# Three order tables of a decoder layer's kernel, arranged anew

## The chip, the cores and the metric

The kernel runs on one core of a Trainium2 chip. A core has a matrix engine (TensorE, "PE" in the profile, with its weight loads shown as "PEld"), a vector engine (VectorE, "DVE"), an activation engine (ScalarE, "ACT"), a general engine (GpSimd, "POOL") and a queue for transfers (SyncE, "SP"). Each runs its own list of instructions in the order in which the program recorded them; they meet at semaphores. The metric is the device time of one execution in microseconds (us).

## The reference

One decoder layer with norms after each part, all in 32-bit floats: 8 sequences of 112 tokens, width 256; a context of 375 rows per sequence.

```
x = layernorm(x + self_attention(x))                # 16 heads of 64
x = layernorm(x + cross_attention(x, ctx, mask))    # 16 heads of 16, 375 keys
x = layernorm(x + moe(x) + shared(x))               # 8 experts, the best one per token

self_attention:  softmax(q k^T / 8) v, then w_out and b_out
cross_attention: softmax(where(mask == 0, -1e10, q k^T / 4)) v, then Wo and bo
moe:    silu(x gate_e^T) * (x up_e^T) down_e^T with e = argmax(x router^T)
shared: the same form with one set of weights for every token
```

## The kernel before

**The work of one sequence** is cut into parts, and each part has a short word. A step `s` (there are 9) runs three sequences at different places: the self attention of sequence `s` (small letters), the cross attention of sequence `s-1` (capitals), and the end of the cross attention of `s-2` (`F1` to `F6`). Between them stand projection pieces for later steps, which depend on nothing that is close in time. The words, with the lines of the code:

| word | part | lines | TensorE's work in it |
|---|---|---|---|
| s0, s1 | self scores of 8 heads, row maxima | 332 | 16 matmuls on 64 rows of the array (row tiles) |
| e0, e1 | subtract the maximum (VectorE), exp (ScalarE) | 350 | none |
| w0, w1 | row sums and reciprocal (VectorE), product (POOL) | 356 | none |
| t00 to t11 | transposes of the self weights, 4 heads, and a copy | 363 | 4, full array |
| v0, v1 | weights times values, and a copy | 371 | 16 on 64 columns (column tiles) |
| o, n | output projection, sum, statistics; normalize | 384, 393 | 16, full |
| q1, q2 | transposes of the normed row block; queries | 406, 410 | 2 and 8, full |
| S0 to S3 | cross scores of 4 heads, minimum and exp of heads 0 and 1 | 433 | 8 on 32 rows |
| E0 to E3 | the same minimum and exp for heads 2 and 3 | 457 | none |
| T00 to T32 | transposes of the cross weights (group, third of the keys), a copy | 460 | 4, full |
| V0 to V3 | cross weights times values, a copy | 470 | 24 on 32 columns |
| F1 to F6 | transposes and division; transposes; output projection, sum, statistics; normalize; transposes for the experts; router scores | 488 to 523 | 4, 2, 4, 0, 2, 4, full |
| k0 to k7 | queries and keys of a pair of sequences | 259 | 8, full |
| u0 to u3 | values of a sequence | 283 | 4, full |
| c0, c1 and c2 to c4 | keys and values of a context | 299 | 4 each, full |
| a0 to a3, b0 to b3 | gate and up of the shared expert, first half of the tokens | 611 | 4 each, full |
| r, R, z | routing on VectorE; ranks and scatter; constants | 666, 680, 214 | R has 4, full |

The counts are those of the profile, where each 32-bit matmul stands twice. A tile that spans all rows and columns of the array is called full here; the others take 32 or 64 rows, or 32 or 64 columns, and put several matmuls side by side.

**The order** is written by hand. The scheduler is off (`tc.manual_schedule()`), and three strings hold the words: `FIRST` for step 0, `STEP` for steps 1 to 7, `LAST` for step 8. The function `step` (lines 532 to 547) reads a string word by word and records the instructions of each part on all engines:

```
for word in table.split():
    on = word[-1] if word[-1] in "+-" else ""
    word = word.strip("+-")
    if word in pieces:
        pieces.pop(word)(on)
        continue
    what, arg = word[0], [int(d) for d in word[1:]]
    whose = {"F": old, "q": crosses.get(s)}.get(what, cross if what in "SETV" else own)
    if whose is not None and what in PARTS:
        getattr(whose, PARTS[what])(on, *arg)
```

A word that has no sequence or piece in a step is left out: no `F` in step 1, no `k` in steps 6 and 7, no `u` in step 7. The sign behind a word says which engine copies the result out of PSUM (line 245): `+` is VectorE, none or `-` is ScalarE. For queries (`k0`, `k2`) and context keys it is always ScalarE, for context values always VectorE.

**Buffers.** Three pools of PSUM have two tiles each: `sc` (scores; S takes both, s one), `pt` (all transposes) and `mm` (all other matmuls). So each group of matmuls waits until the tile of the group but one before it, in its pool, has been read out. The weights `pr`, `ex` and their transposes are doubled too.

**Transfers** are issued on SP in the order of the program. Those that the words touch: the context of the next sequence, at the start of each step, once the buffer's last reader, a `c` piece of the step before, is done; and the weights of the shared expert, after step 7, into memory that the self attention has left.

After step 8 come the end of the last cross attention, the second half of the shared expert, the routing, and nine tiles of experts (from line 708); the tables don't touch them.

Of the kernel before, what the change touches and what calls it, by code (L numbers as in the profile page):

```python
# [25 lines left out]


STEP = """
S0 c0 E0 F1 s0 c1 T00- T01- e0 S1 w0 F2 T02- E1 c2 s1 V0- T10- t00- e1 F3 T12- T11- c3 F4 c4 t01- w1
V1- F5 S2 k0 u0- t10- E2 t11+ S3 v0+ v1+ E3 T20+ T21+ o T22- T30+ F6 u1- k1+ T32- k3- V2- n q1 T31+  # L30
k2 q2 V3+
"""
FIRST = """
k5+ s0 e0 k7+ k6 w0 k4 u2+ s1 t00+ e1 u3+ t01+ k0 w1 c0 u1- v0+ c1 t10+ t11+ k2 v1+ o k1+ n c2 c3 z
q1 u0- q2 k3+ c4
"""
LAST = """
S0 E0 F1 a0- b0- F2 T00+ S1 E1 T01- T02+ F3 a1+ F4 T10- V0+ T12- T11- S2 V1- b1- F5 E2 b3- a2- r
T20- R T22- S3 E3 b2- T21+ a3- T30+ T31+ F6 T32+ V2+ V3+
"""  # L40


# [919 lines left out]
```

## Time and profile before

| | |
|---|---|
| median of 3 runs | 432.33 us (431.8 to 432.77) |
| the profiled execution, its own time | 431.49 us |
| its span, from the first to the last instruction | 429.7 us |
| granted clock of TensorE, mean | 0.992 |
| step 0 (from the first matmul at 5.0) | to 48.6 us |
| step 1 | 48.6 to 86.7 us |
| steps 2 to 5, each | 39.7 us |
| step 6 | 245.6 to 279.5 us |
| step 7 | 279.5 to 311.5 us |
| step 8 | 311.5 to 338.3 us |
| the rest | 338.3 to 429.7 us |

A step is counted from the first matmul of its `S0` to that of the next. The page has these costliest groups (line, engine, operation, out<-in, shapes, count; busy time, mean length in ns; idle time before it on its engine and who ended it):

```profile
L455 ACT ACTIVATE ex<-ex,nm 112x375 f32<-112x375 f32 x128 | 70.5, 601 | 47.8 <-DVE nm L451 47.1
L451 DVE CUSTOM_DVE_ANT_0 ex<-sc,cap 112x375 f32<-112x375 f32 x128 | 63.2, 542 | 19.4 <-PE sc L439 19.4
L465 PE MATMUL pt<-ident,ex 112*125 112x112 f32 x384 | 55.9, 278 | 0.3
L361 POOL TENSOR_TENSOR pr<-pr,den 112x896 f32<-112x896 f32 x16 | 26.9, 1682 | 127.9 <-ACT exT L247 71.9
L247 ACT COPY exT<-pt 125x448 f32<-125x448 f32 x62 | 31.3, 530 | 30.4 <-PE pt L465 30.4
...
L247 DVE COPY exT<-pt 125x448 f32<-125x448 f32 x34 | 20.4, 618 | 19.1 <-PE pt L465 19.0
```

A line is that of the code, or of a helper: every copy out of PSUM has line 247, every plain product line 251. The length of a matmul is modelled and overlaps the next one, so for TensorE the distance from start to start is read, not the sum of lengths. Idle time of an engine that isn't the bound costs nothing.

### The profile page before, as it was taken

The numbers are of one execution on the slowest core, as the hardware profiler recorded it, in microseconds if no ns is written. First come the engines' busy times: TensorE is split into PE (matmuls) and PEld (weight loads), VectorE is DVE, ScalarE is ACT, GpSimd is POOL, SyncE is SP. The second block draws the span as 40 slices with busy tenths as digits, with TensorE's granted clock in tenths as the row PEclk, the third lists the DMA queues.
The fourth block names the chain that finished last, engine by engine and source line by source line (L and its number), as shares of the span: only waits on it lengthen the run. The fifth ranks groups of instructions, "written<-read, shape, count | busy, mean of one in ns | idle before, by whom it ended". The sixth has DMA issues, their size and how long they took to land.

```text
span 429.7 us, 8390 instructions
## 1 busy us (share of the span) xinstructions
PE 411.0 (96%) x3378; PEld 318.7 (74%) x3378; DVE 244.5 (57%) x676; ACT 182.2 (42%) x365; POOL 87.6 (20%) x117
## 2 busy tenths in 40 slices
PE   5999999999999999999999999998999899999990
PEld 4968677877787787778777776766865665899990
DVE  0554676387638655863785387588675745106442
ACT  1221375366437634752664286366356501111110
POOL 3030012103001200221040012113100515713334
PEclk9999999999999999999999999999999999999996
DMA  8970390001000100010010000000395204179700
GB/s 278 300 203 0 116 273 30 1 2 37 2 0 2 38 2 0 4 36 2 1 37 2 2 2 0 2 2 2 122 400 215 66 15 147 32 260 384 271 24 24
DMA packets 27372, 35.80 MB, mean 83 GB/s; under 512 B 2448, under 2 KB 20191, under 8 KB 27330
## 3 DMA queue, kind: packets, MB, share of 16 engines
q1 hardware_dynamic: 25202, 31.94, 22.9%
q0 software_dynamic: 1584, 2.76, 2.0%
q8 instruction: 28, 0.46, 0.4%
q10 hardware_dynamic: 544, 0.52, 0.3%
q14 instruction: 14, 0.11, 0.1%
HBM read 28.78 MB, written 7.62 MB: 85 GB/s over the span
## 4 chain that ended last, share of the span: by engine, by line
PE 94%; DVE 1%; DMA 1%; POOL 1%; issue 1%; ACT 1%; POOLq 0%
PE mm L251 49%; PE pt L465 11%; PE sc L251 10%; PE sc L439 6%; PE mm L476 5%; PE sc L339 3%; PE mm L375 3%; PE pt L368 3%; PE pt L242 2%; DMA wq<-in_w_qkv 1%; PE pt L492 1%; PE pt L823 0%; POOL pr L361 0%; DVE ex L451 0%; POOL rs L232 0%
## 5 line engine op out<-in xcount | busy, mean ns | idle before, releaser
L455 ACT ACTIVATE ex<-ex,nm 112x375 f32<-112x375 f32 x128 | 70.5, 601 | 47.8 <-DVE nm L451 47.1
L451 DVE CUSTOM_DVE_ANT_0 ex<-sc,cap 112x375 f32<-112x375 f32 x128 | 63.2, 542 | 19.4 <-PE sc L439 19.4
L465 PEld LDWEIGHTS pt<-ident,ex 112*125 112x125 f32 x384 | 49.9, 189 | 10.0 <-issue 2.8
L465 PE MATMUL pt<-ident,ex 112*125 112x112 f32 x384 | 55.9, 278 | 0.3
L361 POOL TENSOR_TENSOR pr<-pr,den 112x896 f32<-112x896 f32 x16 | 26.9, 1682 | 127.9 <-ACT exT L247 71.9
L247 ACT COPY exT<-pt 125x448 f32<-125x448 f32 x62 | 31.3, 530 | 30.4 <-PE pt L465 30.4
L232 POOL TENSOR_TENSOR rs<-rs,mhalf 112x1 f32<-112x1 f32 (+1 forms) x25 | 14.3, 571 | 144.3 <-DVE rs L231 144.2
L251 PE MATMUL mm<-xT_sb,wq 128*128 128x224 f32 x128 | 29.0, 373 | 5.0 <-DMA wq<-in_w_qkv 5.0
L247 DVE COPY exT<-pt 125x448 f32<-125x448 f32 x34 | 20.4, 618 | 19.1 <-PE pt L465 19.0
L251 PE MATMUL mm<-wv,xT_sb 128*112 128x512 f32 x64 | 30.5, 599 | 0.0
L251 PEld LDWEIGHTS mm<-xT_sb,wq 128*128 128x128 f32 x128 | 24.3, 199 | 8.0 <-DMA wq<-in_w_qkv 5.0
L439 PE MATMUL sc<-kc,qz 32*112 32x375 f32 x256 | 29.8, 519 | 0.0
L251 PE MATMUL mm<-wo,aoT 128*112 128x256 f32 x128 | 29.0, 380 | 0.0
L251 PE MATMUL mm<-xT_sb,wk 128*128 128x224 f32 x128 | 27.8, 363 | 0.0
L251 PEld LDWEIGHTS mm<-xT_sb,wk 128*128 128x128 f32 x128 | 24.6, 197 | 2.8 <-issue 2.2
L251 PEld LDWEIGHTS mm<-wo,aoT 128*112 128x112 f32 x128 | 22.1, 177 | 4.5
L476 PE MATMUL mm<-exT,vc 125*32 125x112 f32 x768 | 24.8, 263 | 0.0
L251 PE MATMUL mm<-cT,wxk 128*128 128x375 f32 x64 | 24.4, 503 | 0.0
L251 PE MATMUL mm<-wxv,cT 128*125 128x256 f32 x96 | 23.6, 382 | 0.0
L247 DVE COPY kT<-mm 128x448 f32<-128x448 f32 x11 | 6.9, 623 | 25.4 <-PE mm L251 25.4
L354 ACT ACTIVATE pr<-pr 112x896 f32<-112x896 f32 x16 | 15.4, 960 | 13.3 <-DVE pr L353 13.3
L476 PEld LDWEIGHTS mm<-exT,vc 125*32 125x32 f32 x768 | 17.4, 110 | 4.9 <-issue 1.9
(160 smaller groups left out, 664.4 us busy)
## 6 DMA issues: line engine op xcount, KB each, us to landing
wg<-in_gateT SPq DMA_DIRECT2D x9, 512.0 KB, 9.7
wu<-in_upT SPq DMA_DIRECT2D x9, 512.0 KB, 10.5
wd<-in_downT SPq DMA_DIRECT2D x9, 512.0 KB, 10.0
cT<-in_ctxT SPq DMA_DIRECT2D x8, 375.0 KB, 3.3
xs_d<-fill_sb SPq DMA_DIRECT2D x1, 1799.0 KB
zs_d<-fill_sb SPq DMA_DIRECT2D x1, 1792.0 KB
wv<-in_w_qkv SPq DMA_DIRECT2D x2, 512.0 KB
wo<-in_w_out SPq DMA_DIRECT2D x1, 1024.0 KB
```

What stands on the lines that cost most here:

```text
L232: G.tensor_tensor(rs[:n], rs[:n], mhalf[:n], ALU.pow)
L247: (V.tensor_copy if on == "+" else A.copy)(dst, src)
L251: nc.tensor.matmul(out_, lhsT, rhs, start=(i == 0), stop=(i == len(pairs) - 1))
L339: nc.tensor.matmul(sc[:S, j, bass.ts(c, S)], qT[rows, 4 * g + c, self.tok], kT[rows, 4 * g + c, self.tok], start=True, stop=True,)
L354: A.activation(pr, pr, AF.Exp)
L361: G.tensor_tensor(pr, pr, den.unsqueeze(3).to_broadcast([S, 2, 4, S]), ALU.mult)
L368: nc.tensor.transpose(pt[:S, bass.ts(c, S)], self.pr[g][:, j, c, :], ident[:S, :S])
L439: nc.tensor.matmul(sc[i // 2][:S, i % 2, :S2], self.qz[rows, par, c, :], kc[rows, c, :], start=True, stop=True,)
L451: V.tensor_tensor_reduce(ex[:, i, :], self.sc[g][i // 2][:S, i % 2, :S2], cap, -1.0, BIG, ALU.add, ALU.min, nm[:, i : i + 1],)
L455: A.activation(ex[:, i, :], ex[:, i, :], AF.Exp, bias=nm[:, i : i + 1], scale=-1.0)
L465: nc.tensor.transpose(pt[:JT, bass.ts(i, S)], self.ex[g][:, i, bass.ts(t, JT)], ident[:S, :S])
L476: nc.tensor.matmul(av[32 * i : 32 * i + 32, 0:S], vcs[self.b % 2][:, t, 8 * c + 2 * i + par, :], self.exT[g][:, t, bass.ts(i, S)], start=( ...
```

## The change

Only the three strings change. The same words stand in each; their order is another, and some have another sign. In `STEP`, `v0`, `T21`, `T30` and `k1` go from `+` to `-`. In `FIRST`, `k5`, `u2`, `u3`, `v0`, `t11`, `k1` and `k3` go from `+` to `-` and `u1` from `-` to `+`. In `LAST`, `T02`, `a1` and `V0` go from `+` to `-`, and `b0`, `T10`, `V1` and `T20` from `-` to `+`.

```
 STEP = """
-S0 c0 E0 F1 s0 c1 T00- T01- e0 S1 w0 F2 T02- E1 c2 s1 V0- T10- t00- e1 F3 T12- T11- c3 F4 c4 t01- w1
-V1- F5 S2 k0 u0- t10- E2 t11+ S3 v0+ v1+ E3 T20+ T21+ o T22- T30+ F6 u1- k1+ T32- k3- V2- n q1 T31+
-k2 q2 V3+
+S0 c1 E0 s0 c0 T00- e0 k3- F1 S1 T01- T02- E1 c4 s1 V0- F2 e1 u1- w0 T10- c3 w1 T11- c2 T12- S2 V1-
+F3 t00- t01- u0- t10- E2 t11+ k0 v0- F4 v1+ S3 T20+ E3 F5 o T21- T22- F6 k2 T30- V2- n q1 T32- k1-
+T31+ q2 V3+
 """
 FIRST = """
-k5+ s0 e0 k7+ k6 w0 k4 u2+ s1 t00+ e1 u3+ t01+ k0 w1 c0 u1- v0+ c1 t10+ t11+ k2 v1+ o k1+ n c2 c3 z
-q1 u0- q2 k3+ c4
+k6 k5- k7+ u3- k4 s0 e0 s1 k2 e1 u1+ w1 w0 c1 u2- k1- k3- c0 t00+ t01+ c2 t10+ z t11- v0- v1+ o n
+u0- c3 q1 k0 q2 c4
 """
 LAST = """
-S0 E0 F1 a0- b0- F2 T00+ S1 E1 T01- T02+ F3 a1+ F4 T10- V0+ T12- T11- S2 V1- b1- F5 E2 b3- a2- r
-T20- R T22- S3 E3 b2- T21+ a3- T30+ T31+ F6 T32+ V2+ V3+
+S0 E0 b0+ a2- T00+ T02- S1 F1 T01- a0- E1 F2 b3- S2 b1- E2 T10+ F3 T11- a1- r T12- V0- V1+ F4 S3
+T20+ R T22- a3- E3 T21+ F5 b2- T30+ F6 T31+ T32+ V2+ V3+
 """
```

## The prediction, made before the changed kernel ran

> **What bounds the kernel now.** I read the page first (busy shares, chain), then the stretches of one step each, then one step in the timeline, TensorE alone and with all engines.
>
> ```profile
> span 429.7 us, 8390 instructions
> PE 411.0 (96%) x3378; PEld 318.7 (74%) x3378; DVE 244.5 (57%) x676; ACT 182.2 (42%) x365; POOL 87.6 (20%) x117
> PE 94%; DVE 1%; DMA 1%; POOL 1%; issue 1%; ACT 1%; POOLq 0%
> ```
>
> The chain of what ended last lies to 94% on TensorE, so time is won only by what TensorE does between matmuls. By stretches (columns: length; busy us and instructions of PE, PEld, DVE, ACT, POOL; clock; DMA share; GB/s):
>
> ```profile
> 166.10:205.80 39.70, 39.67 (x362) 30.58 (x358) 24.87 (x67) 21.14 (x43) 5.88 (x6) 1.00 0.04 11
> 245.60:279.50 33.90, 33.87 (x334) 24.75 (x330) 24.37 (x66) 19.47 (x40) 5.70 (x6) 1.00 0.00 1
> 279.50:311.50 32.00, 30.50 (x322) 23.36 (x318) 24.31 (x66) 18.50 (x38) 5.69 (x6) 1.00 0.13 42
> ```
>
> A full step takes 39.7 us with TensorE "busy" throughout, but busy is not peak: matmul ends are modelled and overlap. What counts is start to start, in TensorE's timeline (start, length, group):
>
> ```profile
> 131.41 1.02 PE L465 MATMUL pt<-ident,ex 112*125 112x112 f32 x8
> 132.36 1.04 PE L439 MATMUL sc<-kc,qz 32*112 32x375 f32 x8
> 133.34 0.41 PE L242 MATMUL pt<-ident,xo 112*128 112x112 f32 x2
> 134.99 1.04 PE L339 MATMUL sc<-kT,qT 64*112 64x112 f32 x16
> 135.96 0.78 PE L476 MATMUL mm<-exT,vc 125*32 125x112 f32 x24
> 136.68 0.97 PE L465 MATMUL pt<-ident,ex 112*125 112x112 f32 x4
> 137.55 0.59 PE L368 MATMUL pt<-ident,pr 112*112 112x112 f32 x4
> 138.84 1.03 PE L465 MATMUL pt<-ident,ex 112*125 112x112 f32 x8
> 139.71 1.90 PE L251 MATMUL mm<-wxv,cT 128*125 128x256 f32 x8
> 143.81 1.78 PE L251 MATMUL mm<-xT_sb,wq 128*128 128x224 f32 x8
> 145.43 1.88 PE L251 MATMUL mm<-wv,xT_sb 128*112 128x512 f32 x4
> 157.91 1.68 PE L251 MATMUL mm<-xT_sb,wk 128*128 128x224 f32 x8
> 159.42 0.59 PE L465 MATMUL pt<-ident,ex 112*125 112x112 f32 x4
> ```
>
> Two things are to be seen. First, the tile shape costs. Eight projection matmuls between full-array groups take 159.42-157.91 = 1.51 us; entered from a row-tiled group (143.81) they take 1.62: an entry costs 0.11. Leaving costs as much: all single starts around a change of shape show some 0.19 from the last matmul of 112 columns to the next shape's first, where the same shape gives 0.095. Second, eight transposes of ex take 139.71-138.84 = 0.87, so four take 0.44; the four at 136.68 take 0.87. The same moments with all engines:
>
> ```profile
> 134.35 1.08 DVE L359 TENSOR_REDUCE den<-pr 112x8 f32<-112x896 f32 x1
> 136.00 0.55 DVE L451 CUSTOM_DVE_ANT_0 ex<-sc,cap 112x375 f32<-112x375 f32 x1
> 136.12 1.11 ACT L455 ACTIVATE ex<-ex,nm 112x375 f32<-112x375 f32 x2 [0.35 <-DVE nm L451]
> 137.28 0.18 PEld L465 LDWEIGHTS pt<-ident,ex 112*125 112x125 f32 x1 [0.20 <-ACT ex L455]
> ...
> 298.31 0.98 PE L368 MATMUL pt<-ident,pr 112*112 112x112 f32 x8 [1.31 <-POOL pr L361]
> ```
>
> The word w0 (1.08 us of den on VectorE) stands ahead of E1, so the exps of heads 2 and 3 end at 137.23 and T10 has to wait; t00 right after it waits for POOL's product of the same w0. In step 7, which has no k and u pieces to fill, t10 waits 1.31 us for POOL.
>
> **What the Trainium skill says.** "TensorEngine Tiling (Array Packing)", Key Properties: a change of tiling mode, not of tile alone, drains TensorE. The trace agrees: 0.19 in place of 0.095 at each change. "TensorE: Matmul & The Clock Gate", Part 2, step 1: weight loads are pulled ahead of running matmuls, the matmuls keep their order; the page adds (Architectural detail) that ScalarE and VectorE are strict FIFO. Here too: the first pair after a change is longer by a weight load (0.42 against 0.315 for 375 columns), and E1 stands behind den.
>
> **The change part by part.** Arithmetic is unchanged: the same matmuls; by the order of instructions 31 PSUM copies go from VectorE to ScalarE (four in a full step: v0, T21, T30, k1). That is 4 x 0.53 = 2.1 us more on ScalarE (21.1 to 23.3 of 39) and 4 x 0.62 less on VectorE: free in total, only queue order matters.
>
> (a) Tile shapes. Counted in TensorE's order, changes of shape fall from 153 to 141: FIRST 8 to 4 (s0,s1 and v0,v1 become neighbours), six STEP steps by one, LAST by two. One change removed saves exit plus entry, 0.095 plus 0.06 to 0.11, taken as 0.18: 12 x 0.18 = 2.2 us.
>
> (b) w0, w1 go behind E1, u1 and T10, so E1 follows S1's own two heads. I laid the step out anew by adding the start-to-start durations of its groups (S 0.83, keys 1.37, s 0.97, k 1.51, u 1.72, V 0.71, o 3.46, two v 1.69, c vals 0.87, q2 0.97 and so on). From S0 = 0: s0 2.29, T00 4.63, S1 7.11, T01 7.93, c4 8.9, V0 10.8, T10 13.5, S2 16.65, F3 18.2, t00 19.1, u0 19.9, k0 22.4, v0 24.0, S3 25.7, o 27.2, V2 34.0, q1 34.7, T31 36.9, V3 38.3, end 39.04. Against it the producers in their queues: E1's second exp ends 11.7, T10 needs it at 13.5 (0.19 gone); w0's product ends on POOL at 16.3, w1's at 18.5, t00 comes at 19.1 and t10 at 21.6 (0.16 gone). S1 now lies 1.1 us later (7.11, before 132.36-126.34 = 6.0) and clears e0's subtraction (5.6), for which it took 0.98 in place of 0.83 (0.15 gone). So 0.5 us of waits go per step.
>
> (c) Key pieces and norm's steps moved later: c1/c0 swapped, k3 early, F2 to F6 shifted. Norm: o's sum ends 31.2, POOL's power 32.7, n 33.1, q1 at 34.7, covered. On SP only the context load is touched: it waits for the last c piece (now 16 us into a step, before about 15) and lands 3.3 us after issue, needed next step: free. The shared weights wait for o of step 7, land some 5 us after it, and b0 now comes first, 6.3 us after it: margin 1.3. FIRST asks for the second half of wv at about 18 us; SP's ring of semaphores shows it down at 12.6. POOL's queue keeps its kinds of work; the power for F3 comes behind both w products, at 20.6, with F4 at 23: free.
>
> (d) Tight places of the new order: v1 wants k0's PSUM buffer at 24.85, ScalarE frees it at 24.75; V0 wants T02's copy by 11.1, which stands behind S1's exps and ends 10.7; V3 wants T31's copy (38.1) at 38.3. Each lies between nothing and 0.2 us; below nothing it can't go, no work is shorter. I take 0.1 a step in all.
>
> Sum by stretch: FIRST -0.7 (four changes, no other wait before). Step 1: waits 0.15+0.68 (58.5 to 60), change 0.0, less 0.1: -0.75. Steps 2 to 5: 4 x (0.5+0.17-0.1) = -2.3. Step 6: 0.5, 0.16 (q2 behind x1T's copy), change 0.17, less 0.15 new (T31 behind q1's copy): -0.7. Step 7: before 0.5+1.38+0.24+0.16, change 0.17, less 1.0 new (T12 behind T10's copy 0.3; t10 behind t00's copy, which stands behind S2's exps, 0.5; T31 0.2): -1.5. LAST: -0.36 for changes, +0.3 because R, and with it POOL's scatters, come 1.4 us later and b2 is squeezed: -0.1. The tail from 338.3 is the same code and moves along. Sum -6.05. Own time of the profiled execution: 431.49, of which 429.7 is span; so 425.4. The median shown is 432.33, 0.84 above: 426.3.
>
> **Rivals.**
> 1. Only the shapes count: waits move, as exps and copies of ScalarE (2.1 us more per step) end late elsewhere. For: T01, T02 and V0 now stand behind S1's exps in ScalarE's FIFO, and step 7 shows how quickly a thin step waits. Against: ScalarE idles 16 us of a full step. Gain 2.2: 430.1.
> 2. Slower: ScalarE's queue between S1 and e1. T01's and T02's copies stand behind two exps; if VectorE's xo product and S1's maxima ahead of them come late, V0 (10.8) and, behind it, F2, u1 and T10 shift alike in every step. Margin 0.4 us; each further us costs 7 us over seven steps. To eat the gain of 6 takes 0.4+0.86 = 1.26 us of lateness; at 1.7 us, about three more ScalarE items ahead, the time is 432.33 + 7x1.3 - 6 = 435.4. Against: in the trace copies come 0.2 us after their matmuls and 0.41 apart.
> 3. Nothing: the changes of shape are paid but the weight load of the next group would have been exposed anyway, and waits move wholly. 432.3.
>
> **How the numbers follow.** Forecast, waits and changes gone: 0.66 (own range 424.6 to 428). Rival 1: 0.20. Rival 2: 0.09. Rival 3: 0.05. Predicted 426.3. The range 424.0 to 430.8 takes in rival 1's value and the unknown costs of (d), 0.2 us a step. What a measurement can tell from no change is 0.2%, 0.86 us. Faster 0.86, same 0.05, slower 0.09.
>
> **What would show it.** Right: stretches S0 to S0 near 39.1 (39.7), step 7 near 30.5, FIRST ending near 47.8 (48.6); four transposes of T10 in 0.5; no POOL wait over 1 us on TensorE. Wrong: any TensorE group in a full step that lasts 0.3 us over its duration above, above all V0, v1, V3 or T12; a step of 40 us or more; b0 waiting for a DMA.

## The result, and the profile after

The changed kernel takes **425.42 us** (median of 4 runs, 424.85 to 425.79), beside 432.15 us (4 runs, 431.8 to 432.77) of the kernel before: ratio 0.9842, 95% interval 0.9824 to 0.9859, so it is faster by 1.6%. The prediction was 426.3 us, faster. The profiled execution took 425.79 us, 5.7 less than that of before; its span is 424.1 us. The page of the changed kernel:

```profile
span 424.1 us, 8388 instructions
...
PE 406.5 (96%) x3378; PEld 316.6 (75%) x3378; DVE 227.9 (54%) x645; ACT 195.9 (46%) x396; POOL 89.1 (21%) x117
...
PE 94%; DVE 1%; DMA 1%; issue 1%; ACT 1%; POOL 1%; POOLq 0%; ACTq 0%
...
L247 ACT COPY exT<-pt 125x448 f32<-125x448 f32 x75 | 38.2, 528 | 17.8 <-PE pt L465 17.1
```

The chain still lies to 94% on TensorE with the same 3378 matmuls. VectorE has 31 instructions less and ScalarE 31 more: the copies whose sign changed (the `exT` copies on ScalarE go from 62 to 75). ScalarE is now 13.7 us busier, and the share of the chain on it is still 1%. The stretches of a full step, step 6 and step 7, in the columns used before:

```profile
163.30:202.40 39.10, 39.10 (x365) 30.25 (x360) 22.90 (x63) 22.86 (x47) 5.88 (x6) 1.00 0.04 11
241.50:275.10 33.60, 33.42 (x330) 24.57 (x326) 22.92 (x63) 20.67 (x43) 5.70 (x6) 1.00 0.00 1
275.10:306.30 31.20, 30.58 (x325) 23.25 (x321) 22.74 (x63) 19.60 (x41) 5.66 (x6) 1.00 0.14 49
```

From the first matmul of `S0` to the next one's:

| stretch | before | after | difference | predicted |
|---|---|---|---|---|
| to the first `S0` | 48.56 | 48.23 | -0.33 | -0.7 |
| of it, from the fifth `k` piece on | 34.97 | 34.29 | -0.68 | |
| step 1 | 38.05 | 36.97 | -1.08 | -0.75 |
| steps 2 to 5, each | 39.74 | 39.06 | -0.68 | -0.57 |
| step 6 | 33.91 | 33.64 | -0.27 | -0.7 |
| step 7 | 32.07 | 31.18 | -0.89 | -1.5 |
| step 8 (`LAST`) | 26.80 | 26.49 | -0.31 | -0.1 |
| the rest of the span | 91.35 | 91.30 | -0.05 | 0 |

In TensorE's timeline of the changed kernel a full step now has no wait around its cross weights (columns: start, length, group):

```profile
134.14 1.04 PE L339 MATMUL sc<-kT,qT 64*112 64x112 f32 x16
135.11 0.78 PE L476 MATMUL mm<-exT,vc 125*32 125x112 f32 x24
135.82 0.41 PE L242 MATMUL pt<-ident,xo 112*128 112x112 f32 x2
136.07 1.88 PE L251 MATMUL mm<-wv,xT_sb 128*112 128x512 f32 x4
137.79 0.59 PE L465 MATMUL pt<-ident,ex 112*125 112x112 f32 x4
138.21 1.04 PE L251 MATMUL mm<-wxv,cT 128*125 128x256 f32 x4
...
140.91 0.90 PE L439 MATMUL sc<-kc,qz 32*112 32x375 f32 x8
141.74 0.78 PE L476 MATMUL mm<-exT,vc 125*32 125x112 f32 x24
```

The four transposes of `T10` take 138.21-137.79 = 0.42 us where they took 0.87. `S2` and `V1` (140.91, 141.74) stand next to each other, with one change of shape between them; before, the full-array `F5` lay there, and so two. In step 6 and step 7 waits are left; all engines of the changed kernel there (idle time before an instruction and its releaser in brackets):

```profile
271.50 0.41 DVE L236 TENSOR_SCALAR xrec<-r,mv,rs 112x256 f32<-112x256 f32 x1 [0.66 <-POOL rs L232]
...
272.06 0.38 PE L242 MATMUL pt<-ident,xrec 112*128 112x112 f32 x2 [0.18 <-PE mm L476]
...
287.85 0.95 ACT L247 COPY exT<-pt 125x448 f32<-125x448 f32 x2
...
288.41 0.51 PEld L465 LDWEIGHTS pt<-ident,ex 112*125 112x125 f32 x4 [0.52 <-ACT exT L247]
...
292.11 0.97 ACT L247 COPY prT<-pt 112x448 f32<-112x448 f32 x2 [0.25 <-PE pt L368]
...
292.79 0.95 PE L368 MATMUL pt<-ident,pr 112*112 112x112 f32 x8 [0.33 <-ACT prT L247]
```

`q1` starts at 272.06, right after `n` (271.50 to 271.91): start to start it costs 0.25 us more than in a full step, although the bracket names TensorE. `T12` (288.41, its weight loads) and `t10` (292.79) come behind ScalarE's copies of `T10` and `t00`, 0.28 and 0.49 us late by their starts. POOL's wait of 1.3 us is gone from step 7.

### The profile page after: what moved, and what is told of

Read it like the earlier page. It is cut to its first block, busy times and chain, and to the rows that moved or that the text cites. A ratio compares the mean times of both kernels' runs of the same rounds, so it can differ in the third digit from the quotient of the medians.

```text
span 424.1 us, 8388 instructions
## 1 busy us (share of the span) xinstructions
PE 406.5 (96%) x3378; PEld 316.6 (75%) x3378; DVE 227.9 (54%) x645; ACT 195.9 (46%) x396; POOL 89.1 (21%) x117
## 4 chain that ended last, share of the span: by engine, by line
PE 94%; DVE 1%; DMA 1%; issue 1%; ACT 1%; POOL 1%; POOLq 0%; ACTq 0%
PE mm L251 49%; PE sc L251 11%; PE pt L465 10%; PE sc L439 6%; PE mm L476 5%; PE sc L339 4%; PE mm L375 3%; PE pt L368 3%; PE pt L242 2%; DMA wq<-in_w_qkv 1%; PE pt L492 1%; PE pt L823 0%; POOL rs L232 0%; DVE pr L353 0%; DVE mx L348 0%
## 5 line engine op out<-in xcount | busy, mean ns | idle before, releaser
L465 PEld LDWEIGHTS pt<-ident,ex 112*125 112x125 f32 x384 | 52.1, 188 | 17.0 <-issue 12.4
L247 ACT COPY exT<-pt 125x448 f32<-125x448 f32 x75 | 38.2, 528 | 17.8 <-PE pt L465 17.1
L247 DVE COPY exT<-pt 125x448 f32<-125x448 f32 x21 | 13.0, 622 | 27.3 <-PE pt L465 27.2
L251 PE MATMUL mm<-wxv,cT 128*125 128x256 f32 x96 | 24.9, 382 | 0.0
L348 DVE TENSOR_REDUCE mx<-sc 112x8 f32<-112x896 f32 x16 | 17.5, 1091 | 10.0 <-PE sc L339 10.0
```

What stands on the lines that cost most here:

```text
L247: (V.tensor_copy if on == "+" else A.copy)(dst, src)
L251: nc.tensor.matmul(out_, lhsT, rhs, start=(i == 0), stop=(i == len(pairs) - 1))
L348: V.tensor_reduce(self.mx, scv, AX.X, ALU.max)
L465: nc.tensor.transpose(pt[:JT, bass.ts(i, S)], self.ex[g][:, i, bass.ts(t, JT)], ident[:S, :S])
```

## The experiments

The twelve runs, two of them the changed kernel again, lie in four jobs (1 to 4; 5 to 8; 9 and 10; 11 and 12), each job with its own runs of the kernel before. In the second and third job the kernel before took some 16 us more than in the others, and the traces of the kernels in these jobs have more time in step 8 and after it alone; so kernels of different jobs are compared by the lengths of their steps. In those two jobs each kernel also gains 0.8 to 2.7 us less on the kernel before than its shorter first stretch, steps and step 8 add up to; no trace of the kernel before was kept there, so where this goes isn't known. Tables stand as excerpts; `+` is the experiment.

**1. The `STEP` table alone**, with `FIRST` and `LAST` as before.

> Only STEP is the new one, FIRST and LAST are the old ones. Theory (the gain comes from shapes and waits of the seven steps, as the two traces place it): the steps' part of the gain, 1.1+2.7+0.3+0.9 = 5.0 us, ratio 0.9885, a full step of 39.06 us. Rival (step 0 and the last step carry it): less than 2 us.

426.65 us, ratio 0.9899 (0.9859 to 0.9939). Steps 1 to 7 are 37.15, four of 39.06, 33.64 and 31.19 us, those of the whole change but for 0.18 in step 1. `STEP` brings the larger part; `FIRST` (34.97 us from the fifth `k` piece, as before) and `LAST` (26.81) keep their old lengths.

**2. The old table with only `w0` and `t00` later**: does moving the softmax sums behind `E1` take the two waits away?

```
 ...
-e0 S1 w0 F2 T02- E1 c2 s1 V0- T10- t00- e1 F3 T12- T11- c3 F4
+e0 S1 F2 T02- E1 w0 c2 s1 V0- T10- e1 F3 T12- T11- c3 t00- F4
 ...
```

> The old kernel, in STEP alone w0 goes behind E1 and t00 behind c3; not one change of tile shape less. Theory (T10's wait for E1 and t00's for w0's product go, S1's 0.15 and step 7's wait for w1 stay): 0.35 us a full step, 2.4 us in all, ratio 0.9945, a full step of 39.4. Rival (only tile shapes count, waits move): within 0.5 us of before.

It is slower: 435.21 us, ratio 1.0093 (1.0062 to 1.0123), a full step 40.2 us, 0.46 more than before. All engines of this kernel:

```profile
98.18 1.08 DVE L348 TENSOR_REDUCE mx<-sc 112x8 f32<-112x896 f32 x1
...
100.48 0.95 ACT L354 ACTIVATE pr<-pr 112x896 f32<-112x896 f32 x1 [1.17 <-DVE pr L353]
...
101.34 0.95 ACT L247 COPY exT<-pt 125x448 f32<-125x448 f32 x2
...
102.00 0.57 PE L368 MATMUL pt<-ident,pr 112*112 112x112 f32 x4 [0.65 <-ACT exT L247]
```

`T10`'s and `t00`'s old waits are gone, as expected: the group of `T10` takes 0.53 us in place of 0.87. What costs is the new place of `t00`. `e1`'s exp starts on ScalarE at 100.48, behind it stand the copies of `T12` and `T11` (101.34), and `t00` wants the PSUM tile that one of them reads: it starts 0.82 us late by the starts of its neighbours. The same instructions in the kernel before, with `t01` in the last line:

```profile
97.07 1.08 DVE L348 TENSOR_REDUCE mx<-sc 112x8 f32<-112x896 f32 x1
...
99.37 0.95 ACT L354 ACTIVATE pr<-pr 112x896 f32<-112x896 f32 x1 [0.40 <-DVE pr L353]
...
100.23 0.95 ACT L247 COPY exT<-pt 125x448 f32<-125x448 f32 x2
...
101.71 0.55 PE L368 MATMUL pt<-ident,pr 112*112 112x112 f32 x4
```

`S0` of this step is at 86.61 here and at 87.71 in the experiment, so in both kernels `s1`'s maximum, `e1`'s exp and these copies start 10.47, 12.77 and 13.63 us into the step: moving `w0` did not make them later. Before, the next transposes were `t01`, behind `c3` and `c4`, and did not wait. So of the two words moved, `w0` took a wait away and `t00` met a new one. This is the second rival's mechanism, exps ahead of copies, at another place.

**3. The new kernel with shape changes put back**: five more in a full step, 31 in all, with the same groups.

```
 ...
-E1 c4 s1 V0- F2 e1
+E1 c4 s1 F2 V0- e1
 ...
-S2 V1- F3 t00-
+S2 F3 V1- t00-
 ...
-k0 v0- F4 v1+ S3 T20+ E3 F5 o
+k0 F4 v0- F5 v1+ T20+ S3 E3 o
 ...
```

> The new kernel, in STEP F2 stands between s1 and V0, F3 between S2 and V1, F5 between v0 and v1, T20 ahead of S3: 31 changes of tile shape more in seven steps (5 a step, 1 in step 1), the same work. Theory (0.15 to 0.19 us for each): 4.7 to 5.9 us slower than the new kernel, ratio to before about 0.997, a full step of 39.85. Rival (the drain is hidden by weight loads that would wait anyway): within 1 us of the new kernel, ratio 0.985.

430.5 us, ratio 0.9991 (0.9977 to 1.0005). A full step is 39.87 us: +0.81 for five changes, 0.162 each. Steps 6 and 7 pay 1.04 and 0.78 for their five, since `v0` waits there for some 0.3 us more and, in step 7, `T12` for 0.2 us less. TensorE in this kernel, the stretch shown above of the changed one:

```profile
134.07 1.04 PE L339 MATMUL sc<-kT,qT 64*112 64x112 f32 x16
135.05 0.41 PE L242 MATMUL pt<-ident,xo 112*128 112x112 f32 x2
135.39 0.78 PE L476 MATMUL mm<-exT,vc 125*32 125x112 f32 x24
...
137.91 0.59 PE L465 MATMUL pt<-ident,ex 112*125 112x112 f32 x4
```

`F2`'s two transposes stand between `s1` and `V0`, and from `s1` to `T10` it is 137.91-134.07 = 3.84 us, where the changed kernel has 137.79-134.14 = 3.65: the same matmuls, one change more, 0.19 us.

**4. The four old signs**: `v0`, `T21`, `T30` and `k1` copied by VectorE again in the new order.

```
 ...
-v0- F4 v1+ S3 T20+ E3 F5 o T21- T22- F6 k2 T30- V2- n q1 T32- k1-
+v0+ F4 v1+ S3 T20+ E3 F5 o T21+ T22- F6 k2 T30+ V2- n q1 T32- k1+
 ...
```

> The new kernel with the old signs in STEP: v0, T21, T30 and k1 are copied by VectorE again. Theory (the copies lie beside TensorE's work on either engine): within 0.5 us of the new kernel, ratio to before 0.984 to 0.986. Rival (moving copies to ScalarE is what shortened the steps): 2 us or more slower than the new kernel, ratio 0.989 or above.

428.82 us, ratio 0.9946 (0.9927 to 0.9965), where 0.984 to 0.986 was expected: the theory failed. Steps 1 to 7 take 3.9 us more than in the changed kernel; a full step is 39.53 us, +0.47, and steps 6 and 7 are 34.33 and 32.07, +0.69 and +0.89. The rival's number came in; experiments 5 to 7 ask whether for its reason. All engines of this kernel, and below it `n` and `q1` in the changed kernel, one step later:

```profile
158.43 0.62 DVE L247 COPY exT<-pt 125x448 f32<-125x448 f32 x1 [1.39 <-PE pt L465]
158.97 0.41 DVE L236 TENSOR_SCALAR xrec<-r,mv,rs 112x256 f32<-112x256 f32 x1
...
159.43 0.41 PE L242 MATMUL pt<-ident,xrec 112*128 112x112 f32 x2 [0.40 <-DVE xrec L236]
```

```profile
196.26 0.41 DVE L236 TENSOR_SCALAR xrec<-r,mv,rs 112x256 f32<-112x256 f32 x1 [0.66 <-POOL rs L232]
...
198.05 0.41 PE L242 MATMUL pt<-ident,xrec 112*128 112x112 f32 x2
```

With `T30` on VectorE, its copy stands in the queue ahead of `n`, and `q1` waits for `n`. With it on ScalarE, `n` ends at 196.67, 1.4 us before `q1` wants it.

**5 to 7. Which part of it?** `w0` alone back ahead of `E1`; `T30` alone back on VectorE; the other three signs back.

```
 ...
-S1 T01- T02- E1 c4 s1 V0- F2 e1 u1- w0 T10-
+S1 w0 T01- T02- E1 c4 s1 V0- F2 e1 u1- T10-
 ...
```

> The new kernel, in STEP w0 stands behind S1 again, ahead of E1, as in the old order. Theory (w0's 1.3 us on VectorE push E1, c4 and s1's maxima back; in the new order T10 has 1.9 us to spare, so it still does not wait, but u1 waits 0.15 for c4's buffer and c2 and T12 some 0.5 for copies behind e1's exp): a full step of 39.5 to 39.8 us, 3 to 5 us slower than the new kernel in all, ratio to before 0.991 to 0.996. Rival 1 (it is T10's wait that w0 makes): T10 waits 0.2 us again, 39.3. Rival 2 (w0's place is free in the new order): 39.06.

443.32 beside 447.12 us in that job, ratio 0.9926 (0.9891 to 0.9962). A full step is 39.23 us: +0.17, not the 0.4 or more that I expected. Step 7 is 0.45 longer, step 6 0.03. `T10` doesn't wait in any of them. All engines of this kernel:

```profile
137.41 0.95 ACT L354 ACTIVATE pr<-pr 112x896 f32<-112x896 f32 x1 [1.50 <-DVE pr L353]
...
138.27 0.57 ACT L247 COPY v<-mm 112x512 f32<-112x512 f32 x1
...
138.89 1.13 PE L251 MATMUL mm<-wxv,cT 128*125 128x256 f32 x4
```

`e1`'s exp is late, `u1`'s copy stands behind it, and `c2` (138.89), which takes `u1`'s PSUM tile, starts 0.08 us late; `T12` after it is 0.17 late. The expectation had named these two words and taken the cost too large. The old place of `w0` does harm, by ScalarE's queue, but little.

```
 ...
-F6 k2 T30- V2- n q1
+F6 k2 T30+ V2- n q1
 ...
```

> The new kernel, in STEP T30 alone is copied by VectorE again. Theory (n stands behind T30's copy on VectorE, and q1 waits for n): all of what the four old signs cost, a full step of 39.53 us, ratio to before 0.993 to 0.997. Rival (the load on VectorE as a whole): a quarter of it, 39.2.

447.2 us, ratio 0.9996 (0.998 to 1.0012), above the expected 0.993 to 0.997; a full step 39.59 us, +0.53. In a full step this one sign carries all that the four cost in experiment 4, 0.47. In steps 6 and 7 it costs 0.31 and 0.32, less than half of what the four did.

```
 ...
-k0 v0- F4 v1+ S3 T20+ E3 F5 o T21- T22- F6 k2 T30- V2- n q1 T32- k1-
+k0 v0+ F4 v1+ S3 T20+ E3 F5 o T21+ T22- F6 k2 T30- V2- n q1 T32- k1+
 ...
```

> The new kernel, in STEP v0, T21 and k1 are copied by VectorE again and T30 stays on ScalarE. Theory (only T30's copy stands ahead of n): a full step of 39.06 us, within 0.3 us of the new kernel in all, ratio to before 0.984 to 0.987. Rival (load on VectorE): three quarters, 39.4.

443.67 us, ratio 0.9921 (0.9895 to 0.9947); a full step 39.06 us, that of the changed kernel to the hundredth. In a full step the other three signs are free. In steps 6 and 7 they aren't: 33.86 and 31.41 us, +0.22 and +0.23, so the expected 0.3 us in all is missed. All engines of this kernel in step 6:

```profile
268.80 0.53 ACT L247 COPY exT<-pt 125x448 f32<-125x448 f32 x1 [1.74 <-PE pt L465]
...
269.22 0.61 DVE L247 COPY exT<-pt 125x448 f32<-125x448 f32 x1
...
269.38 0.69 PE L465 MATMUL pt<-ident,ex 112*125 112x112 f32 x4 [0.32 <-ACT exT L247]
```

`T21`'s copy (269.22) stands on VectorE behind the sum and the statistics of `o`. The first copy to be done is ScalarE's of `T22`, and `T30` (269.38) starts right after it, 0.44 us later than in the changed kernel, where `T21`'s copy ends first. About half comes back, since `q1` then finds `n` done. In a full step `k2` stands between `T22` and `T30` and covers this; steps 6 and 7 have no `k2`.

**8. A further order**, 17 changes of shape in a full step in place of 18, and a table of its own, `THIN`, for steps 6 and 7, with `T32` ahead of `V2` and of `q1`.

```
 ...
-F3 t00- t01- u0- t10- E2 t11+ k0 v0- F4 v1+ S3 T20+ E3 F5 o T21-
-T22- F6 k2 T30- V2- n q1 T32- k1- T31+ q2 V3+
+F3 t00- t01- k0 t10- E2 t11+ u0- T20+ T21- k2 T22- v0- F4 v1+ V2-
+S3 E3 F5 o T30- T32- k1- n q1 T31+ F6 q2 V3+
 ...
+THIN:  o T21- T22- F6 k2 T30- T32- V2- n q1 k1- T31+ q2 V3+
```

> A further order: in steps 1 to 5 T20 to T22 come ahead of v0, so that v0, v1, V2 and S3 stand together (17 changes of tile shape, not 18), with k0 and u0, T32 and F6 moved to fill; steps 6 and 7 have a table of their own, the new one with T32 ahead of V2 so that n has longer. Theory: 0.18 us a full step less, 38.9, and 0.3 us less in steps 6 and 7 each: 1 to 1.5 us faster than the new kernel, ratio to before 0.981. Rival (a wait takes it back, q2 for x1T's copy or q1 for n): 39.0 to 39.3, no gain.

444.29 us, ratio 0.9926 (0.9901 to 0.995). A full step is 39.31 us, 0.25 more than the changed kernel's, and step 1 is 37.50, 0.53 more; steps 6 and 7 are 33.43 and 30.97, 0.21 less each. All engines of this kernel at the end of a full step:

```profile
160.61 0.41 DVE L236 TENSOR_SCALAR xrec<-r,mv,rs 112x256 f32<-112x256 f32 x1 [0.66 <-POOL rs L232]
...
161.17 0.38 PE L242 MATMUL pt<-ident,xrec 112*128 112x112 f32 x2 [0.23 <-DVE xrec L236]
```

With only `T30`, `T32` and `k1` between `o` and `q1`, the norm (sum, statistics, POOL's power, `n`) isn't done; `q1` comes 0.40 us late by its neighbours' starts and eats the 0.16 gained.

**9 and 10. The same order with a key piece more between `o` and `q1`** (`c2`, taken from between `T11` and `T12`), in `THIN` `F6` later; and the changed kernel again in the same job.

```
 ...
-T11- c2 T12- S2
+T11- T12- S2
 ...
-o T30- T32- k1- n q1 T31+ F6 q2 V3+
+o T30- T32- k1- n c2 q1 T31+ F6 q2 V3+
 ...
-THIN:  o T21- T22- F6 k2 T30- T32- V2- n q1 k1- T31+ q2 V3+
+THIN:  o T21- T22- k2 T30- T32- V2- n q1 k1- T31+ F6 q2 V3+
```

> The new tables, and an order that has one change of tile shape less in a full step (17) and a table of its own for steps 6 and 7; the further order's late norm is mended by putting two key pieces' work (c2, k1) between o and q1. Theory: a full step 38.88 to 38.95 us (0.16 less than the new kernel's 39.06, the price of one change), steps 6 and 7 about 0.4 us less each; 1.2 to 1.8 us less than the new kernel in the same job. Rival: a wait takes it back, q1 for n or T12 for T10's copy (no c2 between T11 and T12 now); then a full step is 39.06 us or more and the two kernels are within 0.5 us.

> The new kernel unchanged, beside the further order on the same chip. Theory: every full step again 39.06 us, steps 6 and 7 again 33.64 and 31.18, FIRST again 34.3 from its fifth key piece to S0; 5 to 7 us less than the kernel before. Rival: the steps depend on the chip, and differ from these by over 0.1 us each.

Full steps take 38.90 us with it and 39.06 again with the changed kernel: the 0.16 of one change, as expected. Steps 6 and 7 gain 0.07 each and not 0.4, and step 1 is 37.20 us, 0.23 longer, so seven steps gain 0.55 us where 1.2 to 1.8 was expected. The times, 442.79 (ratio 0.9895, 0.9873 to 0.9918) and 443.07 us (0.9899, 0.9876 to 0.9922), don't tell the two apart. All engines of the further order, a full step and then step 6:

```profile
158.17 0.41 DVE L236 TENSOR_SCALAR xrec<-r,mv,rs 112x256 f32<-112x256 f32 x1 [0.66 <-POOL rs L232]
...
159.20 0.36 PE L242 MATMUL pt<-ident,xrec 112*128 112x112 f32 x2
...
268.76 1.12 PE L465 MATMUL pt<-ident,ex 112*125 112x112 f32 x8 [0.19 <-ACT exT L247]
```

`n` ends at 158.58, and `q1` starts at 159.20 without a wait. In step 6 nothing is left between `T22` and `T30` once `F6` has gone (there is no `k2`), so `T30` comes to its PSUM tile 0.35 us before ScalarE has read it out.

**11 and 12. Each step with the best table so far**: step 1 with the change's `STEP`, 2 to 5 with that of experiment 9, 6 and 7 with `THIN` of experiment 8; and the changed kernel beside it.

```
-step(s, FIRST if s == 0 else STEP if s < 6 else THIN, pieces)
+step(s, FIRST if s == 0 else ONE if s == 1 else STEP if s < 6 else THIN, pieces)
```

> Each step with the best of the orders tried so far: step 1 the new kernel's table, steps 2 to 5 the further order, steps 6 and 7 the thin table with F6 between T22 and k2. Theory (a step's length hangs on its own table alone): 36.97, 38.90, 33.43 and 30.97 us, in all 1.06 us less than the new kernel; the time 0.8 to 1.3 us less than that of the new kernel on the same chip. Rival: the seam between two tables costs a wait, and one of these steps is over 0.1 us longer than given here.

> The new kernel unchanged, to stand beside c_19 on its chip: full steps 39.06 us, steps 6 and 7 33.64 and 31.18; 6 to 7 us under the kernel before if it is a chip like that of the first runs, 5 to 6 if the part after step 8 is the longer one.

Steps 1 to 7 take 36.98, 38.90 to 38.91, 33.42 and 30.97 us, as expected to 0.01: here a step's length hangs on its own table. That is 1.08 us less than the changed kernel's seven steps in the same job. The times are 424.69 us (4 runs; ratio 0.9838, 0.9811 to 0.9866) and 425.33 us (4 runs; 0.9857, 0.9834 to 0.988). The difference of 0.64 us is less than expected and within the intervals, so as a gain in time it isn't shown; in the traces the shorter steps are, while the first stretch (48.13 against 47.46 us) and the rest (91.62 against 91.29) of those two executions differ the other way.

## Why the prediction was right, and where its terms were off

**The bound and the forecast** held. The traces of the two profiled executions give the sum of the table's differences, -5.6 us of span, against -6.05 predicted. That the sum is so near is partly luck: steps 1 to 5, `LAST` and the rest gained 1.0 us more than predicted and steps 6 and 7 1.0 us less; the 0.4 left lie in the first stretch, whose fifth `k` piece came 0.35 us later. For the profiled execution 425.4 us was predicted and 425.79 measured. The median of 425.42 lies further off because the prediction put it 0.84 above the profiled execution, as with the old kernel; it lies 0.37 below.

**Shape changes**: predicted 12 of them at 0.18 us. The runs give 0.162 (experiment 3), 0.16 (39.06-38.90, experiment 9), 0.17 in the first stretch (0.68 over four, measured from the fifth `k` piece on) and 0.16 in `LAST` (0.31 over two). At 0.162 the twelve make 1.9 us: the first rival, "only the shapes count", would have stopped there. The third, that a change is paid anyway, would have had experiments 3 and 9 show nothing.

**Waits in full steps**: `T10` and `t00` no longer wait, and `S1` takes 0.83 us in place of 0.975, since it comes 7.11 us after `S0`, just where the prediction's layout put it. That is 0.35 and 0.15 us; with one shape change, 0.16, it makes the -0.68. The layout by start-to-start sums holds elsewhere too: every word that part (b) places lies within 0.05 us of its predicted start. The three tight places don't wait: `V0` starts 10.84 us into the step, 0.14 after `T02`'s copy ends, `v1` 0.17 after `k0`'s, `V3` 0.09 after `T31`'s. (`T02` and `T31` are read by later matmuls of `V0` and `V3`, so these two have more room than that.) The reserve of 0.1 a step wasn't needed.

**The reason given for `T10`'s wait holds, but it isn't the only thing that ends the wait.** Part (b) put its end down to `w0` going behind `E1`. In the old order that move does take the wait away: `E1`'s exps end 4.87 us after `S1` before and 4.41 in experiment 2, with `T10` starting 4.31 after `S1` in both. In the new order it isn't needed: with `w0` moved back (experiment 5) the exps end 4.87 us after `S1` again, but `T10` starts 6.41 us after it and doesn't wait. `u1`, 1.72 us and now ahead of `T10`, isn't needed for that either. Step 7 has no `u1`; there `T10` starts 4.84 us after `S1`, its last transpose at 5.17. `S1`, `E1`'s exps and `T10` in step 7 of experiment 5:

```profile
280.50 1.04 PE L439 MATMUL sc<-kc,qz 32*112 32x375 f32 x8
...
284.26 1.11 ACT L455 ACTIVATE ex<-ex,nm 112x375 f32<-112x375 f32 x2 [0.17 <-DVE nm L451]
...
285.34 0.60 PE L465 MATMUL pt<-ident,ex 112*125 112x112 f32 x4
```

The words between `S1` and `T10` are there the old ones (with `c4` for `c2`) and `T01`, 0.53 us, which stood ahead of `S1` before: that is enough. For `t00`'s wait no run parts the causes: `w0`'s product ends at 16.2 us into the step and `t00` now comes at 19.14.

**"Free in total, only queue order matters"** for the copies is right in its form, and experiments 4, 6 and 7 show what it hides: in a full step three of the four signs cost nothing either way, and `T30`'s decides 0.5 us, because `n` stands behind it. In steps 6 and 7 the three cost 0.2 us too, by `T21`'s. "`n` 33.1, `q1` at 34.7, covered" holds with that sign only, and the text didn't say so.

**Step 1** was taken too small (0.75 for 1.08). For the waits of 58.5 to 60 us 0.68 was counted. The groups `T10`, `t00`, `T12` and `T11` took 2.67 us from 58.30 to 60.96 before and take 1.80 after, 0.87 less; and the reserve of 0.1 wasn't needed.

**Steps 6 and 7 were taken too large** by 0.4 and 0.6 us. The four waits that the prediction foresaw there are there: 0.28 at `T12` (predicted 0.3), 0.49 at `t10` (0.5), 0.16 at `T31` in each step (0.15 and 0.2). What failed is the 0.5 of removed waits carried over from the full step, and the cover of `n`. Without the `k3` piece (1.53 us), `S1` comes 5.6 us after `S0` and takes 0.97 us as before, so 0.145 isn't gained; without `k2` and `k1`, `q1` waits 0.25 us for `n`, new in step 6, and in step 7 as large as the 0.24 which the prediction counted as gone. Taken off, step 6 is left with -0.3 and step 7 with -1.1; of the last 0.2 about half is a longer `v` group behind the late `t10`.

**`LAST`** was given +0.3 for the later routing; nothing of it is seen there (-0.31 is its two changes), and the rest of the span kept its length (-0.05), as the prediction had it.

**The Trainium skill's two statements** stand. "TensorEngine Tiling (Array Packing)", Key Properties, has the drain at a change of mode, and its size here is 0.16 us. The strict queues of "TensorE: Matmul & The Clock Gate", Architectural detail, are the mechanism of experiments 2, 4 and 5: there a copy stands behind an exp on ScalarE, or `n` behind a copy on VectorE, and TensorE starts 0.82, 0.47 and 0.17 us later.

## What to carry to other kernels

Where a chain lies on TensorE and orders are free, count the changes of tile shape and price them by one measured pair, but judge every reordering by the in-order queues of ScalarE and VectorE: which exp or copy stands ahead of the one that frees the next tile. A stall that seems to belong to one word may be bought off by another; and a word moved away from one wait can meet another: in the old order moving `w0` and `t00` won 0.35 us a step at `T10` and lost 0.82 at `t00`. Check the thin steps apart, since a table tuned for a full step loses its cover where its filler pieces are missing.

## What the runs showed that I had not expected

**The same steps, another end.** Steps 1 to 7 of one kernel agree to 0.01 us in all three traces of it. Step 8 and the rest don't: 26.49 and 91.30 us in its first trace (26.49 and 91.29 in the fourth job's), 29.26 and 106.78 in the third job's. One of TensorE's waits in the changed kernel (us in total, times, longest), in the third job and then in the first trace:

```profile
PE sc L251 <- ACT xsT L825: 9.7, 1, 9.7
```

```profile
PE sc L251 <- ACT xsT L825: 0.2, 1, 0.2
```

The instruction that is waited for copies rows which come by transfers through memory, and in the chain of waits of the third job 16.61 us stand under "another core or an unknown queue". I read it as these rows arriving late; no run shows why. The 2.8 us more in step 8 lie between the start of its `V3` and the end of the step (3.46 us in place of 0.69). The chip alone is not what sets it: the second and the fourth job ran on the same one, with 447.12 and 431.3 us for the kernel before. What slows this part in some jobs stays open.

**A start that varies.** The time to the fifth `k` piece is 12.4 to 13.9 us over the runs, with one code; this is why the first stretch is compared from there on, and why a difference of 0.7 us between two profiled executions isn't yet one of their tables.
